# A graph layer's aggregation product: three parts by features, or two parts by features and a remainder by nodes that TensorE transposes back

## The chip, the cores and the metric

The kernel runs on one NeuronCore of one Trainium2 chip. The metric is the device time of one execution in microseconds. The kernel before took 565.74 us, the median of three runs (565.58 to 565.81).

The engines that matter here: TensorE multiplies matrices (in the profile PE for matmuls and PEld for the weight loads that precede them), VectorE (DVE) and ScalarE (ACT) work on elements, GpSimd (POOL) helps, SyncE (SP) issues DMAs. A matmul takes a stationary operand of up to 128 x 128 (the weights, loaded first) and streams a moving operand of up to 512 columns past it; the sum lands in a PSUM bank of 128 partitions x 512 fp32.

## The reference

One block of a graph transformer over 1250 nodes with 512 features and 41250 directed edges (self loops among them). The part that is changed lies in the graph network, which has two layers:

```
x = prelu(x @ lin_W.T + lin_b)
for l in range(2):
    agg = segment_sum(x[src], dst)
    h = x + agg
    h = prelu(h @ conv_W1[l].T + conv_b1[l], conv_a[l])
    h = h @ conv_W2[l].T + conv_b2[l]
    h = batch_norm over the nodes, then relu
    x = h
```

Beside it the block has a linear attention ("mix") with its own layer norm, and behind both a gated mixture feed-forward part with a last layer norm.

## The kernel before, in words

The sum over edges is made a matrix product. An adjacency matrix of counts, `adj` (1250 x 1250, source nodes on the partitions in ten tiles of 128, the last of 98, destination nodes along the free axis), is built at the start from one-hot products. Since the product with `conv_W1` is linear, each layer first multiplies the features by `conv_W1` (`y_stage`, lines 991 to 1002, result by nodes) and then sums over the edges (`z_stage`, lines 1004 to 1016). `y` is kept as two fp32r tiles, `y_h` (the value rounded to fp32r) and `y_l` (what the rounding left), which together hold it to about fp32 precision; the counts in `adj` are small whole numbers. So the edge sum of layer l is y_h^T adj + y_l^T adj, accumulated in PSUM.

`z_stage` needs its result by features: z_t holds 128 features per partition block (four blocks, DT = 4) and the 1250 nodes along the free axis, since the next product, `h_stage` (lines 1018 to 1045, with `conv_W2`), contracts over features. `z_stage` goes over three parts of the nodes, `CHUNKS = [(0, 418), (418, 416), (834, 416)]`, and in each over the four feature blocks. One group is 20 matmuls into one bank: ten source tiles, y_h and y_l in turn; the weights are 128 x 128 of y, the moving operand is 418 or 416 columns of adj (line 1012). Behind each group `prelu` (line 625) reads the bank: two ScalarE instructions (lines 618 and 619, the positive side into z_t and the negative into `u`) and one on VectorE that joins them (line 623). Then `between(i)` is called, i from 0 to 11.

In layer 0 `between` is `with_q` (line 1119): it puts into the gaps between groups the work on the attention's queries, one tile of nodes per call: `q_second` (line 1078, VectorE), `q_first` (line 1064, four fp32 matmuls of 512 columns, line 1068, then VectorE and ScalarE) and `q_third` (line 1085, four transposes on TensorE, line 605, and a copy on ScalarE, line 609). In layer 1 `between` does nothing, but for one call that issues a few small VectorE instructions (`test_blocks`).

`h_stage` goes over the four output feature blocks and in each over the three parts `CHUNKS`: four fp32 matmuls (line 576) that read the four feature blocks of z_t at that part's nodes, then ScalarE (line 1025) and VectorE (line 1026). In layer 0 its `between` adds work of the attention (`with_mix`), in layer 1 almost none.

Instructions are issued per engine in an order that a scheduler makes from the order of the program; in these stages TensorE's order is the program's. All PSUM tiles come from one pool of eight banks with one tag (`bank()`, line 562): a new tile takes a bank that has been read out. Temporary rows (`u`, and others) come from a pool with four buffers of the tag "xt". When layer 1's product is done, the space of `adj` is given to weights of the feed-forward part, whose DMAs start then (lines 1145 to 1165).

Of the kernel before, what the change touches and what calls it, by code (L numbers as in the profile page):

```python
# [9 lines left out]
F32 = mybir.dt.float32  # L10
# [7 lines left out]
P = 128  # L18
N = 1250
D = 512  # L20
DT = D // P
NT = 10
# [19 lines left out]
CHUNKS = [(0, 418), (418, 416), (834, 416)]  # L42


def rows(t):
    return min(P, N - t * P)
# [479 lines left out]
def usual_block(  # L526
# [23 lines left out]
    nc = tc.nc  # L550
# [3 lines left out]
    tmp = ctx.enter_context(tc.tile_pool(name="tmp", bufs=2))  # L554
# [7 lines left out]
    def bank(dtype=F32):  # L562
        return psum.tile([P, 512], dtype, tag="bank", name="bank")

    def large(place, shape, dtype=F32, name="large"):

        return big.tile(shape, dtype, tag=place, name=name)
# [10 lines left out]
    ident = const.tile([P, P], F32, name="ident")  # L578
# [23 lines left out]
    def rows_turned(src, n):  # L602
        pt = bank()
        for c in range(DT):
            nc.tensor.transpose(pt[:, c * P:c * P + n], src[:, c * P:(c + 1) * P], ident[0:n, 0:n])
        return pt

    def features(copy, dst, t, pt, n):
        copy(dst[:, :, t * P:t * P + n], pt.rearrange("p (c n) -> p c n", c=DT)[:, :, 0:n])  # L609

    def to_features(dst, t, src, n):

        features(nc.scalar.copy, dst, t, rows_turned(src, n), n)

    def both_sides(dst, ps, cn, bias):

        u = tmp.tile([P, D], F32, tag="xt", bufs=4, name="u")
        nc.scalar.activation(dst, ps[:, :cn], AF.Relu, bias=v(*bias))  # L618
        nc.scalar.activation(u[:, :cn], ps[:, :cn], AF.Relu, bias=minus(*bias), scale=-1.0)  # L619
        return u  # L620

    def joined_sides(dst, u, cn, slope):
        nc.vector.scalar_tensor_tensor(dst, u[:, :cn], minus(*slope), dst, op0=ALU.mult, op1=ALU.add)  # L623

    def prelu(dst, ps, cn, bias, slope):

        joined_sides(dst, both_sides(dst, ps, cn, bias), cn, slope)
# [13 lines left out]
    def v(name, i=0, n=1):  # L641
        at = _COLS[name][0] + i
        return v_sb[:, at:at + n]
# [4 lines left out]
    def minus(name, i=0):  # L648
        at = _COLS[name][0] + i
        return m_sb[:, at:at + 1]  # L650
# [45 lines left out]
    adj_r = apool.tile([P, NT, N], F32R, name="adj")  # L696
    adj = adj_r.bitcast(F32)
    nc.gpsimd.memset(adj, 0.0)
    for t in range(NT):
        n = rows(t)  # L700
# [60 lines left out]
    def lin_sides(i, f):  # L761
        c0, cn = PARTS[i]
        live[i, f] = both_sides(h_t[:, f, c0:c0 + cn], live[i, f], cn, ("lin_b", f))
# [49 lines left out]
    def test_blocks():  # L813

        lo, hi = low[:, 0, :], low[:, 1, :]
        test = tmp.tile([1, 3, NB], F32, tag="row", bufs=3, name="test")
        nc.vector.memset(test, 0.0)
        nc.vector.tensor_tensor(test[:, 0, :], hi, base[0:1, :], ALU.subtract)
        nc.vector.tensor_scalar(test[:, 0, :], test[:, 0, :], float(W), None, op0=ALU.is_ge)
        nc.vector.tensor_tensor(test[:, 1, 0:NB - 1], hi[:, 0:NB - 1], lo[:, 1:NB], ALU.is_gt)  # L820
        nc.vector.tensor_tensor(test[:, 2, 0:NB - SHARED], hi[:, 0:NB - SHARED], lo[:, SHARED:NB], ALU.is_ge)
        nc.vector.tensor_reduce(flags[:, 0:1], test.rearrange("p a b -> p (a b)"), AX.X, ALU.max)
        nc.vector.tensor_copy(unusual, flags[:, 0:1])
# [60 lines left out]
    with given(engines={E.PE, E.DVE, E.Activation}):  # L884
# [3 lines left out]
        for step in HEAD_ORDER.split():  # L888
            name = step.rstrip("0123456789")
# [101 lines left out]
    def y_stage(l, h_t, w1, places, between):  # L991
        y_h = large(places[0], [P, NT, D], F32R, name="y_h")
        y_l = large(places[1], [P, NT, D], F32R, name="y_l")
        for t in range(NT):
            between(t)
            n = rows(t)
            ps = bank()
            for c in range(DT):
                nc.tensor.matmul(ps[:n], h_t[:, c, t * P:t * P + n], w1[:, c, :], start=(c == 0), stop=(c == DT - 1))  # L999
            nc.scalar.copy(y_h[0:n, t, :], ps[:n])  # L1000
            nc.vector.tensor_tensor(y_l[0:n, t, :], ps[:n], y_h[0:n, t, :].bitcast(F32), ALU.subtract)
        return y_h, y_l

    def z_stage(l, ys, place, between):
        z_t = large(place, [P, DT, N], name="z_t")
        for b, (c0, cn) in enumerate(CHUNKS):
            for f in range(DT):
                ps = bank()
                for s in range(NT):
                    n = rows(s)  # L1010
                    for y in ys:
                        nc.tensor.matmul(ps[:, :cn], y[0:n, s, f * P:(f + 1) * P], adj_r[0:n, s, c0:c0 + cn],  # L1012
                                         start=(s == 0 and y is ys[0]), stop=(s == NT - 1 and y is ys[1]))
                prelu(z_t[:, f, c0:c0 + cn], ps, cn, ("b1", l * DT + f), ("conv_a", l))
                between(b * DT + f)
        return z_t

    def h_stage(l, z_t, w2, place, between):
# [35 lines left out]
    ys = y_stage(0, h_t, w1, ("A", "D"), with_blocks)  # L1054
# [64 lines left out]
    def with_q(i):  # L1119
        for step, t in ((q_second, i - 1), (q_first, i), (q_third, i - 2)):  # L1120
            if 0 <= t < NT:
                step(t)

    z_t = z_stage(0, ys, "C", with_q)
    place["x_sb"] = large("B", [P, NT, D], name="x_sb")
    w1 = weight(conv_w1[1], "w1")
# [14 lines left out]
    w2 = weight(conv_w2[1], "w2")  # L1141
    ys = y_stage(1, h_t, w1, ("C", "D"), lambda t: None)
    z_t = z_stage(1, ys, "A", lambda i: test_blocks() if i == 5 else None)
    gw = weight(g1_w, "gw")
    graph.close()
# [31 lines left out]
    turned, live = {}, {}  # L1177
# [117 lines left out]
    for t in range(NT):  # L1295
        n = rows(t)
# [79 lines left out]
    for e in range(NE):  # L1376
        nc.tensor.matmul(sums[1][:, 0:P], gated[e // 2][:, e % 2, :], t1s[e][:, 0, 0:P],
                         start=False, stop=(e == NE - 1))
# [118 lines left out]
def graph_block(tc, *args):  # L1497

    unusual = usual_block(tc, *args)
    with tc.If(unusual > 0):  # L1500
        general_block(tc, *args)
# [58 lines left out]
```

## Time and profile before

| what | value |
|---|---|
| median of three runs | 565.74 us |
| the profiled execution | 568.56 us |
| its span, first to last instruction | 566.1 us |
| mean granted TensorE clock | 0.991 |
| matmuls in all | 2385 |
| line 1012, y_h and y_l | 240 + 240 matmuls, busy 86.5 + 84.4 us, mean record 361 and 352 ns |
| line 618, ScalarE, first side of prelu | 24, mean 608 ns |
| line 623, VectorE, joining the sides | 24, mean 653 ns |

How to read it: a record of a matmul lasts from its issue to the end of its results; records overlap, as the next matmul streams while the last one's results drain. So the busy time of a group counts overlapped time twice when means are multiplied, and the spacing of matmuls is read from their starts. A line of the timeline that ends in xN has merged N like instructions, from the first start to the last end. "idle before" names the time in which an engine stood still ahead of an instruction, and what ended it.

### The profile page before, as it was taken

How to read it: one execution, taken by the hardware profiler on the slowest of the kernel's cores; microseconds unless marked ns; L12 is line 12 of the kernel's file. 1: busy time of each engine (PE TensorE's matmuls, PEld its weight loads, DVE VectorE, ACT ScalarE, POOL GpSimd, SP SyncE). 2: the span in 40 equal slices, each digit the busy share in tenths (PEclk: the TensorE clock that was granted, in tenths of full speed). 3: DMA queues.
4: the chain of work that ended last, by engine and by line, in shares of the span. 5: the costliest groups of instructions: out<-in, count | busy, mean ns of one | idle time of the engine just before them, and what ended most of it. 6: DMA issues, size and time to landing. Idle time of an engine off the chain costs nothing. (4 is left out here: it accounts for less than half of the span.)

```text
span 566.1 us, 6992 instructions
## 1 busy us (share of the span) xinstructions
PE 546.7 (97%) x2385; PEld 368.6 (65%) x2385; DVE 325.4 (57%) x1104; ACT 238.8 (42%) x529; POOL 77.0 (14%) x74
## 2 busy tenths in 40 slices
PE   7999999999999999999999999999999999999892
PEld 6865669799855477777854454459995556865440
DVE  4988999977889635444435434111112248717794
ACT  4955454454443122232334443113224447725553
POOL 7200000000000000000013331000000001105693
PEclk8999999999999999999999999999999999999997
DMA  8501000110040020000311002000008320402013
GB/s 284 185 1 52 24 2 1 22 55 2 2 149 1 0 75 0 1 1 1 117 32 55 19 1 74 0 0 1 2 0 314 94 74 2 148 1 76 0 58 131
DMA packets 19286, 29.12 MB, mean 51 GB/s; under 512 B 1529, under 2 KB 8185, under 8 KB 19240
## 3 DMA queue, kind: packets, MB, share of 16 engines
q1 hardware_dynamic: 19096, 28.52, 15.0%
q8 instruction: 21, 0.34, 0.3%
q14 instruction: 25, 0.20, 0.1%
q10 hardware_dynamic: 144, 0.05, 0.1%
HBM read 26.01 MB, written 2.56 MB: 50 GB/s over the span
## 5 line engine op out<-in xcount | busy, mean ns | idle before, releaser
L1012 PE MATMUL bank<-adj,y_h 128*128 128x416 f32 (+1 forms) x240 | 86.5, 361 | 1.1 <-DVE adj L861 1.1
L1012 PE MATMUL bank<-adj,y_l 128*128 128x416 f32 (+1 forms) x240 | 84.4, 352 | 0.0
L843 DVE TENSOR_SCALAR oh_k<-count,e_d 128x240 f16<-128x240 f16 x324 | 83.4, 276 | 0.3 <-PE bank L850 0.3
L1114 POOL TENSOR_TENSOR m<-m,ls_bc 128x512 f32<-128x512 f32 (+1 forms) x10 | 12.7, 1269 | 443.2 <-ACT m L600 443.2
L999 PE MATMUL bank<-w,h_t 128*128 128x512 f32 (+1 forms) x160 | 70.4, 593 | 0.0
L576 PE MATMUL bank<-z_t,w 128*128 128x416 f32 (+1 forms) x192 | 68.9, 513 | 0.0
L576 PEld LDWEIGHTS bank<-z_t,w 128*128 128x128 f32 x192 | 36.1, 189 | 31.8 <-issue 29.9
L841 DVE TENSOR_SCALAR oh_s<-count,s_lo 128x128 f16<-128x128 f16 x228 | 56.6, 248 | 0.0
L999 PEld LDWEIGHTS bank<-w,h_t 128*128 128x128 f32 (+1 forms) x160 | 29.4, 188 | 34.8 <-issue 34.5
L623 DVE SCALAR_TENSOR_TENSOR z_t<-u,m_sb,z_t 128x416 f32<-128x416 f32 (+1 forms) x24 | 15.7, 653 | 59.7 <-ACT u L619 59.7
L1012 PEld LDWEIGHTS bank<-adj,y_h 128*128 128x128 f32 x240 | 45.1, 188 | 2.6 <-issue 2.1
L1012 PEld LDWEIGHTS bank<-adj,y_l 128*128 128x128 f32 x240 | 45.2, 188 | 1.2 <-issue 0.7
L861 DVE TENSOR_TENSOR adj<-adj,bank 128x240 f32 x81 | 32.4, 400 | 16.2 <-PE bank L850 13.8
L850 PEld LDWEIGHTS <-oh_s 128*128 128x128 f16 x324 | 31.6, 98 | 14.6 <-issue 5.6
L850 PE MATMUL bank<-oh_k,oh_s 128*128 128x240 f16 x324 | 40.6, 266 | 0.0
L618 ACT ACTIVATE z_t<-bank,v_sb 128x416 f32<-128x416 f32 (+1 forms) x24 | 14.6, 608 | 61.5 <-PE bank L1012 61.5
L1026 DVE BATCH_NORM_STATS2 bst<-bank 128x6 f32<-128x416 f32 (+1 forms) x24 | 14.4, 600 | 42.9 <-ACT h_t L1025 42.9
L576 PE MATMUL bank<-xn_t,lw 128*128 128x128 f32 (+3 forms) x128 | 37.7, 446 | 1.3 <-DVE xn_t L609 1.3
L948 PE MATMUL bank<-kk,xn 128*128 128x128 f32 (+1 forms) x320 | 38.4, 275 | 0.0
L948 PEld LDWEIGHTS bank<-kk,xn 128*128 128x128 f32 (+1 forms) x320 | 37.0, 192 | 0.1
L1095 PE MATMUL bank<-mixer,q_t 128*128 128x512 f32 (+1 forms) x80 | 36.3, 592 | 0.0
L576 PE MATMUL bank<-xn_t,gw 128*128 128x256 f32 (+2 forms) x128 | 35.3, 427 | 0.9 <-ACT xn_t L609 0.9
(183 smaller groups left out, 794.4 us busy)
## 6 DMA issues: line engine op xcount, KB each, us to landing
t<-in_tv_w SPq DMA_DIRECT2D x12, 512.0 KB, 8.0
w<-in_conv_w SPq DMA_DIRECT2D x4, 1024.0 KB, 5.5
x_in<-in_x SPq DMA_DIRECT2D x9, 256.0 KB, 4.7
xt<-in_x SPq DMA_DIRECT2D x9, 256.0 KB, 4.1
out<-m SPq DMA_DIRECT2D x9, 256.0 KB, 2.8
rest<-in_tv_w SPq DMA_DIRECT2D x4, 512.0 KB, 4.7
lw<-in_lin_w SPq DMA_DIRECT2D x4, 256.0 KB, 5.6
wk<-in_w_qkv SPq DMA_DIRECT2D x1, 1024.0 KB, 6.6
```

What stands on the lines that cost most here:

```text
L576: nc.tensor.matmul(ps[:, :cn], lhs(c), rhs(c), start=(c == 0), stop=(c == k - 1))
L618: nc.scalar.activation(dst, ps[:, :cn], AF.Relu, bias=v(*bias))
L623: nc.vector.scalar_tensor_tensor(dst, u[:, :cn], minus(*slope), dst, op0=ALU.mult, op1=ALU.add)
L841: nc.vector.tensor_scalar(oh_s[:, j, :], count16[:, 0:P], s_lo[:, b, j:j + 1], None, op0=ALU.is_equal)
L843: nc.vector.tensor_scalar(oh_k[:, j, :], count16, key[:, b, j:j + 1], None, op0=ALU.is_equal)
L850: nc.tensor.matmul(ps[:, 0:NT * W], oh_s[:, j, :], oh_k[:, j, :], start=(j == 0), stop=(j == J - 1))
L861: nc.vector.tensor_tensor(adj_r[:, :, at], adj[:, :, at], live.pop(("block", b))[:, 0:NT * W].rearrange("p (s d) -> p s d", s=NT), ALU.add)
L948: nc.tensor.matmul(ps[:, c * P:(c + 1) * P], xn[0:n, t, c * P:(c + 1) * P], k_nodes(f)[0:n, t, :], start=(t == 0), stop=(t == NT - 1))
L999: nc.tensor.matmul(ps[:n], h_t[:, c, t * P:t * P + n], w1[:, c, :], start=(c == 0), stop=(c == DT - 1))
L1012: nc.tensor.matmul(ps[:, :cn], y[0:n, s, f * P:(f + 1) * P], adj_r[0:n, s, c0:c0 + cn], start=(s == 0 and y is ys[0]), stop=(s == NT - 1 a ...
L1026: nc.vector.bn_stats(st[:, b, :], ps[:, :cn])
L1095: nc.tensor.matmul(ps[:n], q_t[:, h, t * P:t * P + n], mixer[:, h, :], start=(h == 0), stop=(h == DT - 1))
```

## The change

`z_stage` no longer goes over the three parts of `CHUNKS`. The first 1024 nodes are done by features as before, in two parts of 512 nodes: eight groups of 20 matmuls with 512 columns of `adj` moving. The last 226 nodes (tiles 8 and 9, of 128 and 98 nodes) are done by nodes: the weights are the 128 or 98 columns of `adj` for these destinations, the moving operand is a whole row block of y, 512 features, and the sum has nodes on the partitions. ScalarE copies such a sum to a row `zn`, TensorE transposes it in four pieces into two banks `turned` (two feature blocks in each, 226 columns a block), and `prelu` reads these banks into z_t.

The order of the groups and of the calls of `between` is written out. The twelve calls remain, with calls 8 and 9 one behind the other; the two groups by nodes stand third and fifth, each turned back one group later; the prelus of the turned sums stand behind the first group of the second part. `h_stage` and its three parts are as before.

```
+    FULL = 2 * D // P
...
     def z_stage(l, ys, place, between):
         z_t = large(place, [P, DT, N], name="z_t")
-        for b, (c0, cn) in enumerate(CHUNKS):
+        c9 = FULL * P
+        turned = []
+        def summed(ps, m, cn, out_of):
+            for s in range(NT):
+                for y in ys:
+                    lhs, rhs = out_of(rows(s), s, y)
+                    nc.tensor.matmul(ps[:m, :cn], lhs, rhs, start=(s == 0 and y is ys[0]),
+                                     stop=(s == NT - 1 and y is ys[1]))
+        def by_features(b, f):
+            c0 = b * D
+            ps = bank()
+            summed(ps, P, D, lambda n, s, y: (y[0:n, s, f * P:(f + 1) * P], adj_r[0:n, s, c0:c0 + D]))
+            prelu(z_t[:, f, c0:c0 + D], ps, D, ("b1", l * DT + f), ("conv_a", l))
+        def by_nodes(t):
+            m = rows(t)
+            ps = bank()
+            summed(ps, m, D, lambda n, s, y: (adj_r[0:n, s, t * P:t * P + m], y[0:n, s, :]))
+            zn = tmp.tile([P, D], F32, tag="xt", bufs=4, name="zn")
+            nc.scalar.copy(zn[:m], ps[:m])
+            return zn
+        def turn_back(t, zn):
+            if not turned:
+                turned.extend((bank(), bank()))
+            m, at = rows(t), t * P - c9
             for f in range(DT):
-                ps = bank()
-                for s in range(NT):
-                    n = rows(s)
-                    for y in ys:
-                        nc.tensor.matmul(ps[:, :cn], y[0:n, s, f * P:(f + 1) * P], adj_r[0:n, s, c0:c0 + cn],
-                                         start=(s == 0 and y is ys[0]), stop=(s == NT - 1 and y is ys[1]))
-                prelu(z_t[:, f, c0:c0 + cn], ps, cn, ("b1", l * DT + f), ("conv_a", l))
-                between(b * DT + f)
+                c0 = f % 2 * (N - c9) + at
+                nc.tensor.transpose(turned[f // 2][:, c0:c0 + m], zn[0:m, f * P:(f + 1) * P], ident[0:m, 0:m])
+        by_features(0, 0)
+        between(0)
+        by_features(0, 1)
+        between(1)
+        zn = by_nodes(FULL)
+        between(2)
+        by_features(0, 2)
+        between(3)
+        turn_back(FULL, zn)
+        zn = by_nodes(FULL + 1)
+        between(4)
+        by_features(0, 3)
+        between(5)
+        turn_back(FULL + 1, zn)
+        by_features(1, 0)
+        between(6)
+        for f in range(DT):
+            c0 = f % 2 * (N - c9)
+            prelu(z_t[:, f, c9:N], turned[f // 2][:, c0:c0 + N - c9], N - c9, ("b1", l * DT + f), ("conv_a", l))
+        between(7)
+        by_features(1, 1)
+        between(8)
+        between(9)
+        by_features(1, 2)
+        between(10)
+        by_features(1, 3)
+        between(11)
         return z_t
```

## The prediction

> **What bounds the kernel now.** I read the totals of the page first, to see which engine could be the bound at all.
>
> ```profile
> span 566.1 us, 6992 instructions
> PE 546.7 (97%) x2385; PEld 368.6 (65%) x2385; DVE 325.4 (57%) x1104; ACT 238.8 (42%) x529; POOL 77.0 (14%) x74
> ```
>
> TensorE is busy 97% of the span. Whether that holds in the stage that changes is asked of the busy time in two stretches: 200 to 290 us holds the product of layer 0 (with the q work between its groups; its last matmul starts at 283), 379 to 425 us that of layer 1 (alone).
>
> ```profile
> 200.00:290.00 90.00, 90.00 (x376) 66.61 (x375) 38.10 (x63) 27.05 (x46) 0.00 (x0) 1.00 0.10 34
> 379.00:425.00 46.00, 46.00 (x243) 45.25 (x242) 7.87 (x12) 12.76 (x23) 0.00 (x0) 1.00 0.00 1
> ```
>
> PE (second number) fills both without a gap, at a granted clock of 1.00; VectorE has 7.87 and ScalarE 12.76 us of work in the 46 of layer 1, no DMA to speak of. So in both stages time is TensorE time, one for one: what counts is how often TensorE starts a matmul, not how long a record is (a record of 0.35 us overlaps the next by half). The timeline gives the starts. Columns: start, duration, engine, line, operation.
>
> ```profile
> 379.76 0.35 PE L1012 MATMUL bank<-adj,y_h 128*128 128x418 f32 x1
> ...
> 424.75 0.35 PE L1012 MATMUL bank<-adj,y_l 98*128 98x416 f32 x1
> 424.93 5.41 PE L576 MATMUL bank<-z_t,w 128*128 128x418 f32 x15
> 425.13 0.61 ACT L618 ACTIVATE z_t<-bank,v_sb 128x416 f32<-128x416 f32 x1 [2.69 <-PE bank L1012]
> 425.64 0.60 ACT L619 ACTIVATE u<-bank,m_sb 128x416 f32<-128x416 f32 x1
> 426.27 0.65 DVE L623 SCALAR_TENSOR_TENSOR z_t<-u,m_sb,z_t 128x416 f32<-128x416 f32 x1 [0.54 <-ACT u L619]
> ```
>
> The first is matmul 3 of the 240 of layer 1, the second the last: (424.75 - 379.76) / 237 = 189.8 ns from start to start, at 416.7 columns on average. The rows below give the same for other kinds, as (merged time - one record) / (count - 1).
>
> ```profile
> 264.06 3.60 PE L1068 MATMUL bank<-wq,xn_t 128*128 128x512 f32 x8
> 267.49 0.60 PE L605 MATMUL bank<-ident,q 128*128 128x128 f32 x4
> 267.85 0.43 PE L1012 MATMUL bank<-adj,y_h 128*128 128x416 f32 x1
> 268.12 0.36 PE L1012 MATMUL bank<-adj,y_l 128*128 128x416 f32 x1
> ...
> 134.23 0.57 PE L850 MATMUL bank<-oh_k,oh_s 128*128 128x240 f16 x4
> ```
>
> Plain fp32 at 512 columns: (3.60 - 0.592) / 7 = 430 ns; at 418 columns (the 5.41 above, record 0.514): 350 ns. That is 0.84 ns per column, or two passes of 0.42 ns, with nothing fixed left over. The fp16 product of 240 columns: (0.57 - 0.266) / 3 = 101 ns, one pass of 0.42 ns. An fp32r matmul of 416.7 columns at one pass should by these rows take 175 ns; it takes 189.8. **Each fp32r matmul costs 14.8 ns more than its columns, and what that depends on decides this case.**
>
> **The change part by part.**
>
> 1. *The products.* Removed in each layer: 12 groups of 20 matmuls at 416.7 columns, 100,000 columns. Added: 8 groups by features (2 parts of 512 nodes) and 2 by nodes (128 and 98 nodes as weights, 512 features moving), 10 groups of 20 at 512: 102,400 columns. Two layers: 480 starts at 189.8 ns = 91.1 us go, 400 starts at 512 columns come. The trace has no fp32r matmul of 512 columns. From below: 512 x 0.42 = 215 ns, no extra at all. From above: the extra grows with the columns, 189.8 x 512 / 416.7 = 233.2 ns. I take a fixed extra, 215 + 14.8 = 229.8 ns, because of these rows at the start of layer 0, where TensorE had been idle:
>
> ```profile
> 199.66 0.19 PEld L1012 LDWEIGHTS bank<-adj,y_h 128*128 128x128 f32 x1 [1.33 <-issue]
> 199.70 0.43 PE L1012 MATMUL bank<-adj,y_h 128*128 128x418 f32 x1 [1.09 <-DVE adj L861]
> 199.77 0.19 PEld L1012 LDWEIGHTS bank<-adj,y_l 128*128 128x128 f32 x1
> 199.96 0.35 PE L1012 MATMUL bank<-adj,y_l 128*128 128x418 f32 x1
> 199.96 0.19 PEld L1012 LDWEIGHTS bank<-adj,y_h 128*128 128x128 f32 x1
> ```
>
> Every weight load in the steady run starts as the matmul before it begins to stream. So the first matmul streamed from 199.77, 0.11 us after its load began, and until 199.96, which is 0.19 us. Weights are usable 0.11 us after a load starts (the record of 0.19 notwithstanding), so the next matmul, whose load began at 199.77, was not waiting for weights at 199.96: the stream itself is stretched, while one load of 128 columns runs beside it. One load per matmul of either width: the extra is likelier per matmul than per column. 400 x 229.8 = 91.9 us: **+0.8 us**, though 80 matmuls fewer are issued.
>
> 2. *Turning back.* 16 transposes. Four in a row (267.49): (0.60 - 0.272) / 3 = 0.109 us each, 1.7 us as an upper bound, as eight of them are only 98 nodes wide. After transposes the first fp32r matmul takes 0.27 instead of 0.19 us, since its load can't hide behind a short stream: twice in layer 1, 0.16 us; in layer 0 the turns stand behind the transposes of q, which pay that already, and one such place goes. Together **+1.8 us**, all on TensorE, in the open.
>
> 3. *The rest.* The two copies of sums by nodes (512 elements on ScalarE, 0.59 us by the q copy) and the prelus (8 of 512 and 4 of 226 for 12 of 416 per layer) lie on engines with at least 33 of 46 us free in layer 1 and 52 of 90 in layer 0. Behind each copy TensorE has a group of 20 x 0.23 = 4.6 us before the turn that waits for it, so nothing. The two banks of turned sums are held for about two steps of the loop; six others remain for three per step in layer 0, where a step is 4.6 + 1.7 (q) + 0.4 us and a bank is read out within 2 us: nothing. In layer 0 the ninth and tenth q steps now follow each other without a group between; in the issue order VectorE's q_second for the tile that the later turn needs stands ahead of the prelu of that group, so no wait, at most 0.5 us. No DMA moves; the loads into the adjacency's space start when the last product ends, as now.
>
> 4. *The last prelu.* h_stage's second piece (nodes 418 to 833) now needs the group that ends last, where so far only the third did. Now it ends at 426.92, 2.17 us after the last matmul started; at 512 elements, scaled from the three rows, some 2.6. The cover is 0.23 + 7 matmuls of 0.35 = 2.68 us in layer 1 (a product of the mixer, 1.7 us, more in layer 0). It just holds: 0, at most 0.3 us.
>
> Sum: +0.8 + 1.8 = **+2.6 us**. The profiled execution took 568.56 us (span 566.1 and 2.5 around it), 2.8 over the median of 565.74; by its own account 568.56 becomes 571.2, by the median 565.74 becomes **568.3**.
>
> *A rule against the rows.* The Trainium skill (TensorE: Matmul & The Clock Gate, section "Back-to-back issue gap") gives a warm matmul N / 2.4 + 2.5 ns: 176 at 416.7 columns, where the trace has 189.8, so the row decides. By the page on both sides the products would go from 84.5 to 86.3 us, +1.8, which with the turning is +3.6: it speaks against the change as well, as it counts columns. The same page (section "Part 4: PE-mode transpose") has about 275 ns for a transpose in a kernel; the record here is 0.272, but the start to start 0.109 us. By the page 16 would be 4.4 us.
>
> **The rivals.** What a measurement can tell here is about 0.2%, 1.1 us.
>
> A. *Fixed extra, as above*: 568.3. Chance 0.50.
>
> B. *The extra goes with the columns* (the moving operand itself streams slower in fp32r): 400 x 233.2 = 93.3, +2.2 + 1.8 = +4.0 us, **569.8**. For it: no fp32r row shows what a stream does without a load beside it. Against: 240 columns of fp16 stream at full rate. Chance 0.27.
>
> C. *The other side: the extra is a floor set by the weight load.* The load's record is 0.19 us, and starts come every 0.19 us, which looks like a bound that 512 columns would hide. Then 400 x 215 = 86.0, -5.1 + 1.8 = -3.3 us, **562.5**. It decides from a start to start of (91.1 - 1.8) / 400 = 223.2 ns downward. For it: the likeness of the two numbers. Against: the rows at 199.66, and q's transposes, whose records of load and matmul are longer than their 0.109 us. Chance 0.10.
>
> D. *A wait at a seam*: the last prelu misses its cover in layer 1, or the adjoining q steps hold TensorE; on top of A at most 0.3 + 0.5 + 0.3, to 569.4, on top of B 570.9. Chance 0.05.
>
> E. *Between A and C*, 221 to 226 ns: -0.9 to +1.1 us, 564.8 to 566.8, no change that can be told. Chance 0.08.
>
> **How the numbers follow.** Slower: A, B and D, 0.82. Same: E, 0.08. Faster: C, 0.10. The time is A's, 568.3; its own range, with 3 ns on the start to start (1.2 us) and the 0.3 of the prelu, is 567.1 to 569.8. The range given holds both bounds of the one unknown cost, from C to B with a wait: 562.5 to 570.9.
>
> **What the changed profile would show.** Step 1: in 46 us of layer 1 the starts of fp32r matmuls about 0.23 us apart (B: 0.233, C: 0.215), the record near 0.39. Step 2: four transposes of zn in 0.60 us, the next matmul's start 0.27 later. Step 3: TensorE still busy through both stretches, the waits for the copies of zn on ScalarE's side alone. Step 4: no idle time at z_t's second piece. Wrong I would be if the starts come below 0.223 us, or if TensorE shows gaps at the turned banks.

## The result, and the profile after

The changed kernel took 570.58 us (median of four executions, 570.32 to 570.82), the kernel before 565.66 beside it: 4.9 us more, a ratio of 1.0081 with a 95% interval of 1.0066 to 1.0096. Slower, as forecast, and inside the range, but nearly twice the 2.6 us of the sum. Its profiled execution took 570.32 us.

The totals of the changed kernel's page, and the busy time in its two product stretches (PE is the second number, the granted clock the last but two):

```profile
span 568.5 us, 6871 instructions
PE 549.7 (97%) x2321; PEld 353.2 (62%) x2321; DVE 324.6 (57%) x1104; ACT 239.9 (42%) x533; POOL 76.6 (13%) x74
```

```profile
198.00:283.00 85.00, 85.00 (x325) 56.10 (x324) 36.27 (x61) 24.17 (x44) 0.00 (x0) 1.00 0.09 31
379.00:426.00 47.00, 47.00 (x208) 37.67 (x207) 7.51 (x12) 13.09 (x26) 0.00 (x0) 1.00 0.00 1
```

64 matmul records fewer (80 products less, 16 transposes more), yet TensorE is busy longer. It fills both stretches, 85.00 of 85 and 47.00 of 47: no wait came with the turned banks, the copies or the adjoining q steps. So whatever the stage lost, it lost in matmuls. The timeline of layer 1 (start, duration, engine, line):

```profile
379.19 0.40 PE L1018 MATMUL bank<-adj,y_l 128*128 128x512 f32 x1
...
396.87 0.39 PE L1018 MATMUL bank<-adj,y_l 98*128 98x512 f32 x1
397.10 0.60 PE L1041 MATMUL bank<-ident,zn 128*128 128x128 f32 x4
397.46 0.48 PE L1018 MATMUL bank<-y_h,adj 128*98 128x512 f32 x1
397.78 0.39 PE L1018 MATMUL bank<-y_l,adj 128*98 128x512 f32 x1
...
425.53 0.40 PE L1018 MATMUL bank<-adj,y_l 98*128 98x512 f32 x1
425.76 4.72 PE L576 MATMUL bank<-z_t,w 128*128 128x418 f32 x13
425.96 0.69 ACT L620 ACTIVATE z_t<-bank,v_sb 128x512 f32<-128x512 f32 x1 [3.38 <-PE bank L1018]
...
427.26 0.75 DVE L625 SCALAR_TENSOR_TENSOR z_t<-u,m_sb,z_t 128x512 f32<-128x512 f32 x1 [0.70 <-ACT u L621]
```

- The first row is matmul 4 of the layer and the second matmul 80: (396.87 - 379.19) / 76 = 232.6 ns from start to start. The prediction took 229.8; its rival B said 233.2.
- Four transposes come (0.60 - 0.272) / 3 = 0.109 us apart, and the next fp32r matmul takes 397.78 - 397.46 = 0.32 us instead of 0.23.
- The last prelu ends at 428.01, 2.48 us after the last matmul started (2.6 estimated), and TensorE does not wait for it.

From the first to the last start of a product the trace has 85.30 us in layer 0 (83.76 before) and 47.42 in layer 1 (45.77): +1.54 and +1.65, **3.2 us together**. Every later trace of either kernel in which the products were left alone repeats these four lengths within 0.04 us. In this execution more was lost behind both products: from the last product's last start to the end of the span the changed kernel took 142.95 us, the kernel before 141.38. The place is the output product (columns of the stretches as above):

```profile
534.74:538.15 3.41, 1.63 (x4) 0.55 (x4) 3.41 (x6) 0.83 (x2) 3.25 (x4) 1.00 0.00 0
538.15:541.56 3.41, 3.41 (x5) 1.34 (x5) 1.72 (x4) 0.08 (x1) 3.41 (x4) 0.50 0.00 0
```

The granted clock was 0.50 for 3.41 us. The first nine matmul records behind the longer wait in the timeline of the changed kernel and, in the second fence, of the kernel before:

```profile
537.90 5.83 PE L1475 MATMUL bank<-m,a_t 128*128 128x512 f32 x9 [1.40 <-POOL m L1405]
```

```profile
537.05 4.13 PE L1421 MATMUL bank<-m,a_t 128*128 128x512 f32 x9 [1.37 <-POOL m L1351]
```

5.83 - 4.13 = 1.70 us. Nothing in the diff touches this code.

And the kernel before? Its profiled execution was 2.8 us over its median. It had such a dip too, in the head, and the changed kernel's had none there. First the kernel before, then the changed kernel, each with its first sixteen matmul records on x from the timeline (start, duration):

```profile
6.88:10.29 3.41, 1.64 (x11) 1.17 (x11) 2.00 (x8) 1.60 (x4) 3.41 (x1) 1.00 1.09 325
10.29:13.70 3.41, 3.36 (x15) 3.37 (x16) 1.04 (x6) 2.28 (x5) 3.41 (x1) 0.50 1.05 374
10.34 3.64 PE L576 MATMUL bank<-xn_t,lw 128*128 128x128 f32 x16 [1.28 <-DVE xn_t L609]
```

```profile
5.67:9.08 3.41, 2.16 (x16) 1.44 (x14) 2.37 (x8) 2.28 (x5) 3.41 (x1) 1.00 1.14 333
9.08:12.50 3.42, 3.04 (x27) 3.04 (x28) 1.92 (x8) 3.12 (x9) 3.42 (x1) 1.00 1.06 362
9.46 2.05 PE L576 MATMUL bank<-xn_t,lw 128*128 128x128 f32 x16 [0.41 <-DVE xn_t L609]
```

The dip cost 3.64 - 2.05 = 1.6 us. Another 0.9 us was lost ahead of it: these matmuls began at 10.34 instead of 9.46 us, because VectorE had waited for a DMA of x until 8.80 instead of 7.92 us (line 738, 740 after the change). The kernel before then stood 2.5 us behind. So the two first profiles differ by 3.2 us of products, +1.7 of a dip in the one's tail, -1.6 of a dip in the other's head and -0.9 of its later x: 2.4 us of span, and 1.8 us of time.

### The profile page after: what moved, and what is told of

Read it like the earlier page. It is cut to its first block, busy times and chain, and to the rows that moved or that the text cites. A ratio compares the mean times of both kernels' runs of the same rounds, so it can differ in the third digit from the quotient of the medians.

```text
span 568.5 us, 6871 instructions
## 1 busy us (share of the span) xinstructions
PE 549.7 (97%) x2321; PEld 353.2 (62%) x2321; DVE 324.6 (57%) x1104; ACT 239.9 (42%) x533; POOL 76.6 (13%) x74
## 5 line engine op out<-in xcount | busy, mean ns | idle before, releaser
L1018 PE MATMUL bank<-adj,y_h 128*128 128x512 f32 (+1 forms) x160 | 64.6, 404 | 1.1 <-DVE adj L863 1.1
L1018 PE MATMUL bank<-adj,y_l 128*128 128x512 f32 (+1 forms) x160 | 63.0, 394 | 0.0
L625 DVE SCALAR_TENSOR_TENSOR z_t<-u,m_sb,z_t 128x512 f32<-128x512 f32 (+1 forms) x24 | 15.1, 651 | 63.5 <-ACT u L621 63.5
L620 ACT ACTIVATE z_t<-bank,v_sb 128x512 f32<-128x512 f32 (+1 forms) x24 | 14.5, 613 | 53.9 <-PE bank L1018 53.9
L576 PE MATMUL bank<-xn_t,lw 128*128 128x128 f32 (+3 forms) x128 | 36.1, 429 | 0.4 <-DVE xn_t L609 0.4
L1122 PE MATMUL bank<-wq,xn_t 128*128 128x512 f32 (+1 forms) x80 | 36.0, 592 | 0.0
L576 PE MATMUL bank<-xn_t,wk 128*128 128x416 f32 (+1 forms) x96 | 35.6, 513 | 0.0
```

Of the source, the lines that this page charges most:

```text
L576: nc.tensor.matmul(ps[:, :cn], lhs(c), rhs(c), start=(c == 0), stop=(c == k - 1))
L1018: nc.tensor.matmul(ps[:m, :cn], lhs, rhs, start=(s == 0 and y is ys[0]), stop=(s == NT - 1 and y is ys[1]))
L1122: nc.tensor.matmul(ps[:n], xn_t[:, c, t * P:t * P + n], wq[:, c, :], start=(c == 0), stop=(c == DT - 1))
```

## Experiments

Three questions: what stretches an fp32r matmul, what turning costs, and whether the dips of the clock belong to the change. "Before" in a result means the kernel before on the same chip.

**The changed kernel and the kernel before once more** (no edit).

> The changed kernel once more, to see whether its tail always loses time. Theory T (a dip of the granted clock): in the first trace of the changed kernel TensorE was granted 0.5 of its clock from 538.1 to 541.6 us, in the output product, which cost 1.7 us of the 4.9; the kernel before showed such a dip not there but at 10.3 us. T expects 570.5 us, and a dip in the tail again in this profile, with the last product's matmuls 0.86 us apart for 3.4 us. Rival R (the dip belongs to that one execution): 570.5 us as well, but a trace without the dip in the tail, and then 1.7 us lost at some other place.

> The kernel before once more: 565.7 us. Its first profiled execution took 568.56, 2.8 over the median. T expects a trace whose granted clock has no dip before the last 8 us, with the first aggregation product at 197.2 us instead of 199.7 and a span near 563.5. R expects dips at varying places, and a span that varies with them.

Measured: 570.75 us (569.17 to 571.22) for the changed kernel against 566.36 (565.14 to 568.59), 1.0070 (1.0051 to 1.0089); 566.46 (565.56 to 568.14) for the kernel before against itself, 1.0003 (0.9987 to 1.0018). Theory T failed in part for the changed kernel: this execution (569.47 us) shows no dip before the end. Nor did it lose 1.7 us elsewhere, as R has it: it is 1.3 us under the median. The kernel before showed one where T had expected none, again in the head (567.06 us). In the changed kernel the stretch ahead of the output product now held more work (first fence); in the kernel before the head's did not (second fence):

```profile
534.88:538.29 3.41, 2.10 (x5) 0.49 (x3) 3.38 (x6) 1.47 (x3) 3.25 (x3) 1.00 0.00 0
538.29:541.70 3.41, 2.95 (x7) 1.44 (x8) 2.45 (x6) 0.10 (x1) 3.41 (x4) 1.00 0.00 0
```

```profile
5.59:9.00 3.41, 1.63 (x13) 1.16 (x12) 2.02 (x8) 2.10 (x4) 3.41 (x1) 1.00 1.11 325
9.00:12.42 3.42, 3.41 (x15) 3.01 (x16) 1.35 (x7) 1.92 (x5) 3.42 (x1) 0.50 1.06 358
```

What follows is the rule that the two kernels share. The stretches shown are the clock's own windows of 3.41 us, counted from the change points of the granted clock. Where TensorE was busy 1.63 or 1.64 us of a window, the next was granted 0.50; where it was busy 2.10 us or more, 1.00. Gone through for all 13 traces of this case, up to the end of the output product, the line is sharp: of the windows at full clock, all six with 1.64 us or less of matmul records were followed by a dip, and all others, from 1.67 us up, were not. Both kernels have two places in which a window can come out so low, the head (TensorE waits for x) and the output product (waits of 0.39 and 1.40 us). Whether it does depends on where the windows lie against the program, which moves from execution to execution, and in the head on when x comes. The line holds for windows at full clock only: with parts of 418, 512 and 320 nodes (next experiment) a window at half clock with 2.27 us of records was followed by a second at 0.50.

**Other widths, all by features.**

```
-        for b, (c0, cn) in enumerate(CHUNKS):
+        for b, (c0, cn) in enumerate([(0, 418), (418, 512), (930, 320)]):
```

> The product by features as before, but in parts of 418, 512 and 320 nodes: the same 480 matmuls and 100,000 columns per layer, no work by nodes, no turning. Fixed extra per matmul (14.8 ns): starts 149, 190 and 230 ns apart at 320, 418 and 512 columns. Extra in proportion to the columns: 146, 190 and 233 ns. A floor set by the weight load: 190, 190 and 215 ns. In the first two cases the time is that of the kernel before, 565.7 within 1 us; with the floor 4.4 us more.

The second kernel of this kind has `[(0, 448), (448, 480), (928, 322)]`.

> The product by features in parts of 448, 480 and 322 nodes. In the run with 418, 512 and 320 nodes the starts were 191, 234 and 149 ns apart: 0.418 ns per column from 320 to 418, but 0.46 from 418 to 512. If the fixed extra of 15 to 16 ns holds up to near 512 and only the full bank costs more: 203 and 216 ns at 448 and 480. If the extra rises with the columns from 418 on: 205 and 219.

Measured: 567.27 us (566.11 to 570.56), 1.0016 (0.9998 to 1.0035) against 566.36, and 567.32 in a single execution; the products took 84.04 + 45.99 and 83.84 + 46.03 us, 0.5 and 0.3 us more than the 83.76 + 45.77 of the kernel before. The groups of the first kernel by form (count, busy time, mean record):

```profile
L1012 PE MATMUL bank<-adj,y_l 128*128 128x512 f32 x72 | 28.5, 396 | 0.0
...
L1012 PE MATMUL bank<-adj,y_l 128*128 128x418 f32 x72 | 25.4, 353 | 0.0
...
L1012 PE MATMUL bank<-adj,y_l 128*128 128x320 f32 x72 | 21.3, 310 | 0.0
```

The record is the start to start and 162 ns more, at each width. Medians of the starts, from the timelines of four kernels:

| columns | start to start, ns | columns at 0.42 ns | extra | 0.4555 ns per column |
|---|---|---|---|---|
| 320 and 322 | 148 | 134, 135 | 13 to 14 | 146, 147 |
| 416 and 418 | 190, 191 | 175, 176 | 15 | 189, 190 |
| 448 | 205 | 188 | 17 | 204 |
| 480 | 218 | 202 | 16 | 219 |
| 512 | 233, 234 | 215 | 18 to 19 | 233 |

The extra grows with the columns, from 13 ns at 320 to 19 at 512. A fixed extra would give 230 at 512, where 233 to 234 were measured, and a floor 190 at 320, where 148 were. 0.4555 ns per column (the 189.8 at 416.7) hits every width within about 2 ns. At 320 columns 148 lies between its 146 and the 149 of a fixed extra, so a small fixed part is not excluded. In the main it is a slower stream, as rival B has it; why an fp32r stream is slower no run here tells.

**Half of the weights.**

```
-                        nc.tensor.matmul(ps[:, :cn], y[0:n, s, f * P:(f + 1) * P], adj_r[0:n, s, c0:c0 + cn],
+                        k = P if (s == 0 and y is ys[0]) or (s == NT - 1 and y is ys[1]) else P // 2
+                        nc.tensor.matmul(ps[:k, :cn], y[0:n, s, f * P:f * P + k], adj_r[0:n, s, c0:c0 + cn],
```

> The kernel before with 64 columns of y as weights in 18 of the 20 matmuls of each aggregation group (the first and the last keep 128), 416 and 418 columns moving: half of the features of each block get no sums, so part of the computation is left out. It asks what stretches an fp32r matmul by 15 ns over its columns. If the weight load that runs beside the stream does (a load of 64 columns is half as long), the starts come 7 to 8 ns closer, about 182 ns, and a layer's product gets 1.6 us shorter. If the stream itself is slower, as a rate or as a fixed cost of each matmul, they stay at 190.

The largest of its groups by form:

```profile
L1013 PE MATMUL bank<-adj,y_l 128*64 128x416 f32 x144 | 50.5, 351 | 0.0
```

The record of y_l was 351 ns with 128 columns of weights as well. At 416 columns the starts come every 188 ns, 190 before (means 188.9 and 189.4), and the products take 83.64 and 45.63 us, 0.12 and 0.14 less, not 1.6. The record of a load fell from 188 to 135 ns, so not to half as the expectation had it, but by far more than the starts moved. The weight load beside the stream is not what stretches it. This takes away the argument by which the prediction had chosen A.

**Turning twice.**

```
+                for _ in range(2):
                     nc.tensor.transpose(turned[f // 2][:, c0:c0 + m], zn[0:m, f * P:(f + 1) * P], ident[0:m, 0:m])
```

> The changed kernel with each of the 16 transposes issued twice. If turning costs what its starts say, 0.109 us each at 128 nodes and about 0.085 at 98, this adds 1.5 us: 572.1. If transposes are hidden or cost their record of 0.27 us each, it adds 0 or 4.4 us. If the time of the tail hangs on the phase of the clock's window, the time may move by 1.7 us either way from 572.1.

Measured: 572.74 us (570.80 to 574.53), 1.0111 (1.0088 to 1.0135) against 566.36; beside the 570.75 of the changed kernel 2.0 more. The products took 86.22 and 48.17 us, 0.92 and 0.75 more than in the first trace of the changed kernel (0.88 and 0.75 more than in its second). Eight transposes in a row in its timeline:

```profile
398.63 1.04 PE L1042 MATMUL bank<-ident,zn 128*128 128x128 f32 x8
```

(1.04 - 0.272) / 7 = 0.110 us each. So turning is in the open and costs some 1.6 us, about half of the 3.2; the wider products cost the other half.

**TensorE's idle places filled**, in both kernels: more idle transposes behind the turns of x in the head, and small matmuls into a bank that is overwritten later, between the first two matmuls of the output product.

```
-            if step == "t0":
-                for i in range(3):
+            if step in ("t0", "t1"):
+                for i in range(8):
...
-        last[t] = bank()
+        last[t] = ahead.pop() if ahead else bank()
         for f in range(FT):
+            if (t, f) == (0, 1):
+                ahead.append(bank())
+                for _ in range(5):
+                    nc.tensor.matmul(ahead[0][:, 0:P], ident, ident, start=True, stop=True)
```

> The kernel before with work that nobody reads put into TensorE's idle places: 8 transposes of the identity instead of 3 behind the first turn of x and 8 more behind the second (at 7 to 10 us), and 5 small matmuls into a bank that is overwritten later, between the first two matmuls of the output product (at 536 us). Theory T (idle windows bring the granted clock down to 0.5 for 3.4 us, 2.5 us lost in the head or 1.7 in the tail): no dip before the end, no run near 568, all within 1 us of 565.4. Rival R (the spread comes from the loads): the spread of 565.1 to 568.6 stays.

> The changed kernel with the same filling. T: no dip, 569.2 us as the two fastest runs of the changed kernel, so 3.6 above the filled kernel before, of which the products and turns explain 3.2 (1.5 to 1.6 in each layer). R: 570.7, as unfilled.

Measured: the kernel before filled took 566.38 us (565.64 to 567.43), 0.9991 (0.9967 to 1.0014) against 566.57 (565.21 to 571.59); the changed kernel filled 569.75 (568.76 to 570.36), 1.0052 (1.0033 to 1.0070). Neither trace has a dip before the end, and of the 24 executions none lies more than 1.1 us over its median. T's "within 1 us of 565.4" was missed all the same: 565.64 to 567.43 us is half of the spread that R names, so R is right in part. Dips do not make all of this rest (567.38 us came at a mean granted clock of 0.994); a later x, as above, may. The recorded executions of the unfilled kernel before fit this: the 35 with a mean granted clock of 0.993 or more, which no trace with a dip ahead of the end reaches, took 565.14 to 567.30 us, median 566.05; the other 31 have a median of 568.02. The filling costs some 0.4 us itself (its fastest run against the fastest of the kernel before), so the kernel before gains nothing that can be told. Between the two filled kernels are **3.4 us**, near the 3.2 that the traces give the products and turns.

**The two fillings apart.** In the changed kernel the output product alone, then the head alone; in the kernel before the output product alone.

```
 (changed kernel, output product alone: the head as it was)
-            if step in ("t0", "t1"):
-                for i in range(8):
+            if step == "t0":
+                for i in range(3):
 (changed kernel, head alone: none between the output product's matmuls)
-                for _ in range(5):
+                for _ in range(0):
```

> The changed kernel with the filling in the output product alone. Theory T2: what the changed kernel loses beyond its products and turns is a dip of the granted clock in the output product, which comes whenever one window of 3.41 us holds both of TensorE's waits there (0.39 and 1.4 us), and the changed kernel's later end puts them into one window in most executions. T2: the runs at 570.6 to 571.2 go, 569.4 median, none below a clock of 0.992 but for dips in the head. Rival: the dips are those of the head (7 to 14 us), and filling the tail leaves 570.7.

> The changed kernel with the filling in the head alone. T2: the dip in the tail stays in most runs, 570.7 median, with runs at a clock of 0.991 or 0.992. Rival (dips of the head): 569.4 and no run above 570.

> The kernel before with the filling in the output product alone. T2: its slow executions near 568 are dips in the head, so they stay, about one in three, and the others remain at 565.2 to 566.6: 566.4 median. Rival: its slow executions are dips in the tail, so none stays above 567.2.

Measured, against 567.46 us: 569.99 (568.78 to 571.74), 1.0049 (1.0029 to 1.0068); 569.76 (569.27 to 571.48), 1.0054 (1.0034 to 1.0073); 567.32 (565.80 to 569.22), 1.0005 (0.9984 to 1.0027). Theory T2, a dip in the tail in most executions of the changed kernel, fell: with the head alone filled six of seven executions stayed at 570.0 or below (the unfilled changed kernel was not run beside them). The trace of that run has both waits in one window and still no dip:

```profile
535.50:538.91 3.41, 1.67 (x4) 0.30 (x2) 3.38 (x7) 1.13 (x2) 3.25 (x4) 1.00 0.00 0
538.91:542.33 3.42, 3.39 (x8) 1.63 (x9) 2.45 (x5) 0.39 (x2) 3.42 (x3) 1.00 0.00 0
```

With the tail alone filled the trace has a dip in the head (10.3 to 13.7 us, 571.74). For the kernel before it held that the dips of the head remain: six of twelve executions over 567.4 with the tail filled. So dips in the head are shown in both kernels, the dip in the tail in one trace of the changed kernel only; that it can strike the kernel before is not shown. Why all four first executions of the changed kernel came out above 570.3 is not settled. One of them is shown to have had the dip in the tail; the other three have no trace, and one of these, at 570.45 us, had no dip ahead of its end: its mean granted clock of 0.995 leaves some 6.2 us of half clock at most, the end of every trace alone takes 5.7 to 8.8, and a dip would add 3.4.

## Why the prediction was right or wrong

- **The bound.** Right: TensorE fills both stretches before and after, and no wait took the place of anything.
- **Step 1, the products (+0.8).** The sign was right, more columns for fewer matmuls, and the term was too small, because its account of the extra was wrong. The matmul of 512 columns starts every 232.6 ns in the steady groups, about 232.2 on average over both layers, not 229.8: 400 x 232.2 - 480 x 189.8 = +1.8 us where the prediction had +0.8. What failed is the choice of the fixed extra. The rows at 199.66 did speak against a wait for weights, but the step from "a load runs beside it" to "the load stretches it" was not in them; half of the weights left the stretch as it was. Rival B's 233.2 was the closer, and its price for the products, +2.2, a little high.
- **Step 2, turning (+1.8).** Right: 1.6 us by doubling it, in the open. The 4.4 us that the prediction had estimated from the 275 ns of the Trainium skill (TensorE: Matmul & The Clock Gate, Part 4: PE-mode transpose) would have been far off.
- **Step 3, the rest (0).** Right in its result. One of its numbers was wrong: a plain fp32 matmul leaves two records (320 records at the k gathering of 160 matmuls), so the q products of a step take 3.4 us, not 1.7, and the banks had more time than stated.
- **Step 4, the last prelu (0).** Right, and with more cover than stated, for the same reason: 14 records of 0.35 us stand before the matmul that needs it, not 7.
- **The sum.** +2.6 predicted; +3.2 in the traces' products, +3.4 between the filled kernels; +4.9 and +4.4 between the plain kernels' medians. The last 1 to 1.7 us have no term in the prediction at all. In the profiled execution of the changed kernel a dip of the granted clock in the output product cost 1.7 us; for its other executions the cause stays open. So it is partly luck that 570.58 us lies inside the range, 0.3 us under its top: the top stood for rival B with a wait, and no wait came. The prediction named the 2.8 us by which the profiled execution exceeded the median, and did not ask where they were; the granted clock (0.50 from 10.3 to 13.7 us) would have told of 1.6 of them, and that such dips decide a microsecond or two of any comparison of this kernel.
- **Rival C** (faster) was excluded by the starts at every width; **D and E** did not come about.

## What to carry to other kernels

Count columns first, and price a matmul by its start to start at the width it will have: in fp32r a wider matmul saved nothing here, since the stretch goes mostly with the columns, so fewer matmuls over 2.4% more columns were a loss before the turning was added. Ask of a layout that needs turning whether TensorE is the bound: here it was, and all 16 transposes were paid in the open at about 0.1 us each. Before a difference of a few microseconds is explained by an edit, look at the granted clock of both profiles for windows at half speed.

## What the runs showed of the hardware

- From start to start an fp32r matmul of this kernel takes 0.455 to 0.463 ns per column (320 to 512 columns), plain fp32 0.84 in each of two records, fp16 0.42 (240 columns). The fp32r stretch, 8 to 10% over 0.42, hardly depends on the width of the weights (64 or 128 columns: mean 188.9 and 189.4 ns).
- As the prediction reads the rows at 199.66, weights are usable 0.11 us after their load starts, although its record lasts 0.19. This rests on taking the start of the next load for the start of a stream; no experiment tested it.
- The granted clock falls to 0.50 for a whole window of 3.41 us when TensorE's records fill 1.64 us or less of the window before (six of six), and doesn't from 1.67 us up: about half. Waits of 0.39 and 1.40 us in one window were enough once (1.63 us of records) and not enough another time (1.67). One such window cost 1.7 us in the tail and 1.6 in the head.
- The Trainium skill (TensorE: Matmul & The Clock Gate, Part 1: The HAM clock gate) describes free-running windows of about 3.4 us with half the clock after an idle one. The traces agree in the length (3.41 us) and the clock (0.50), but the windows ahead of the dips were not idle: five of the six had 1.63 or 1.64 us of records. The advice of the same page (section "Why this matters for your kernels") to have no idle gaps over about 3 us is too lax here, where no wait was longer than 1.40 us in the window ahead of the dip in the tail.
